# Moving the exponent tables of a two-layer spectral convolution to another stage, and the mirror differences to another engine

## The chip, the cores and the metric

The kernel runs on one core of a Trainium2 chip. The metric is the device time of one execution in microseconds (us). The core's engines are TensorE (PE; its weight loads are listed as PEld), VectorE (DVE), ScalarE (ACT), GpSimd (POOL) and SyncE (SP), which here only issues DMA transfers. All data is float32. L265 and the like are line numbers of the kernel before.

## The reference

Two layers act on x of shape 16 images x 16 channels x 256 x 256. The first normalizes groups of two channels and convolves (a 3x3 circular convolution); the second normalizes again and applies a Laplace-type operator, given by poles and residues: a steady part that mixes channels in the frequency domain, and a transient part built from exponentials along y and x.

```python
# layer 0
x = x + _L0_conv_ref(_gn(x), L0_conv_weight)
# layer 1
x = x + _L1_conv_ref(_gn(x), ty, tx, weights_pole1, weights_pole2, weights_residue)

def _L1_conv_ref(x, ty, tx, weights_pole1, weights_pole2, weights_residue):
    alpha = jnp.fft.fft2(x, axes=(-2, -1))
    A = 1.0 / (omega1[:, None, None, None] - weights_pole1[None])
    Bm = 1.0 / (omega2[:, None, None, None] - weights_pole2[None])
    S = jnp.einsum('ikpq,oikp,xikq->oxik', weights_residue, A, Bm)
    output_residue1 = jnp.einsum('biox,oxik->bkox', alpha, S)
    C = jnp.einsum('biox,oikp->bikpx', alpha, A)
    D = jnp.einsum('bikpx,xikq->bikpq', C, Bm)
    output_residue2 = jnp.einsum('bikpq,ikpq->bkpq', D, weights_residue)
    x1 = jnp.fft.ifft2(output_residue1, s=(Ny, Nx), axes=(-2, -1)).real
    E1 = jnp.exp(weights_pole1[..., None] * tyc)
    E2 = jnp.exp(weights_pole2[..., None] * txc)
    F = jnp.einsum('kbpq,bipz->kbiqz', output_residue2, E1)
    x2 = jnp.einsum('kbiqz,biqx->kizx', F, E2).real
    return x1 + x2 / Nx / Ny
```

E1 and E2 are the exponent tables of the change. They depend on the poles and on ty and tx alone, and the first place that reads them is the last stage of the kernel.

## The kernel before

The kernel has four stages. Each engine has its own queue of instructions, which it works through in order; within a queue the order follows the Python code closely, though the framework may move an instruction ahead of one that is not ready.

**Convolution.** The loop over `g` at L642 makes 24 steps for each of the 16 images, 387 in all. A step (`conv`, L251) issues 16 matmuls of 32x32 tiles at L265, recorded as 32. Every six steps a unit (`u`, four an image) of the layer's output, called v, is complete: ACT evicts its four row groups from PSUM with a bias at L280 into the `vt` tiles, of which there are four. Two steps later `mirror` (L230) forms the sum of the upper and the mirrored lower rows into `vsum` (two tiles; L232, DVE, which also accumulates the mean) and the difference in place (L235, DVE). ACT squares both for the variance (L243) four and five steps after `mirror`, and three steps after it SP stores both to `vD` in DRAM (L292, four transfers a unit). These delays are the numbers added to `g` in the lists `folded` and `squared`.

Beside this run the statistics of the images to come (`x_stats`, L159, bn_stats on DVE at L166, with due steps written out), the loads of x (`load_x`, L120: half an image in one transfer, issued by SP after steps 3 and 15 of an image for two images ahead, into five tiles), and two chains of table work: `make_poles`, `make_hat` (twice) and `make_c`, a piece every second step, and `make_exps` (twice) followed by `make_coef`, a piece every fourth step. `make_hat` and `make_c` have matmuls on PE (L443, L605).

**make_exps** (L473) makes a table for two channels at a time, in eight rounds: the phases on POOL (L490), their reduction to the range of the sine by rounding (L492 to L495, POOL) and subtraction in three parts (L501, DVE) and clamping (L504, L505, DVE), the exponentials on ACT (L491), the sine on ACT (L507), the product and two folds on POOL (L509, L511), and one or two stores to `eD` (L516). Exponential and sine need different activation tables, so each round has two loads of a table on ACT.

**Fold and forward transform.** 64 units of v are loaded (`load_v`, L694; the first by POOL, the others by SP), folded on DVE and POOL (L708 to L723) and transformed by PE (L730, L738, L773); spectra go to `aD`.

**Mixing.** The loop at L1109 runs over 32 groups of frequencies `g`, with four slots `n` each. A slot has the sums that make the weights of the next group (PE L981, evicted by ACT L996 and DVE L997), four blocks of 16 mixing matmuls (L1063, recorded as 64 a slot) into four PSUM banks `ps_mix`, their evictions into `yt` (L1120: three on ACT, one on DVE), the loads of the next group's spectra (`load`, L1037, four transfers in three slots of four) and the stores of `yt` to `yD` (`store`, L1075, four transfers). There are two `yt` tiles. `weights` (L918) makes the next weights on DVE and POOL (L952), a piece a slot. After group 2 `unmix_first` borrows a `yt` tile for the first group's repair.

**Inverse transform.** The last stage reads `yD`, `vD` and the tables in `eD`, and writes the output.

Of the kernel before, what the change touches and what calls it, by code (L numbers as in the profile page):

```python
# [9 lines left out]
FP = mybir.dt.float32  # L10
AF = mybir.ActivationFunctionType
# [13 lines left out]
def conv_then_laplace_kernel(ctx: ExitStack, tc: tile.TileContext, a: dict, out: bass.AP):  # L25
# [81 lines left out]
    p1 = ExitStack()  # L107
    wp = p1.enter_context(tc.tile_pool(name="conv_w", bufs=1))
    xp = p1.enter_context(tc.tile_pool(name="xt", bufs=5))
    vp = p1.enter_context(tc.tile_pool(name="vt", bufs=4))  # L110
    fp = p1.enter_context(tc.tile_pool(name="v_sums", bufs=2))
    jp = p1.enter_context(tc.tile_pool(name="junk", bufs=1))
    sp = p1.enter_context(tc.tile_pool(name="stats", bufs=2))
# [116 lines left out]
    def mirror(g, b, u, lo, hi):  # L230
        both = fp.tile([P, 2, 2, N], FP, name="vsum", tag="vsum")
        nc.vector.scalar_tensor_tensor(  # L232
            both, lo, 1.0, hi, ALU.mult, ALU.add, accum_out=sums[:, b, u : u + 1]
        )
        nc.vector.tensor_tensor(lo, lo, hi, ALU.subtract)  # L235
# [214 lines left out]
    def make_coef():  # L450


        rs = sw.tile([P, C, 4, 2], FP, name="s_rs", tag="s_th")
        nc.sync.dma_start(out=rs, in_=a["res_kq"])
        yield
        yield
        u = sw.tile([P, 4, C, 4], FP, name="s_u", tag="s_rn")
# [15 lines left out]
    def make_exps(which):  # L473


        pl = sw.tile([P, C, 2], FP, name="s_pl", tag="s_pl")
        nc.sync.dma_start(out=pl, in_=a[f"pole_e{which + 1}"])
        t = sw.tile([P, N], FP, name="s_t", tag="s_t")
        nc.sync.dma_start(out=t, in_=a[("ty", "tx")[which]].to_broadcast([P, N]))
        sign, phase, turns = (cols[:, 2 + 3 * which + j : 3 + 3 * which + j] for j in range(3))  # L480
        pim = sw.tile([P, C], FP, name="s_pim", tag="s_pim")
        nc.vector.tensor_scalar(pim, pl[:, :, 1], sign, None, ALU.mult)
        yield
        for q in range(8):
            th = sw.tile([P, 2, N], FP, name="s_th", tag="s_th")
            rn = sw.tile([P, 2, N], FP, name="s_rn", tag="s_rn")
            ex = sw.tile([P, 2, N], FP, name="s_ex", tag=f"s_ex{q % 2}")
            for j in range(2):
                i = 2 * q + j
                nc.gpsimd.tensor_scalar(th[:, j], t, pim[:, i : i + 1], None, ALU.mult)  # L490
                nc.scalar.activation(ex[:, j], t, AF.Exp, scale=pl[:, i, 0:1])  # L491
            nc.gpsimd.tensor_scalar(rn, th, 1.0 / (2 * PI), turns, ALU.mult, ALU.add)  # L492
            magic = 1.5 * 2.0**23
            nc.gpsimd.tensor_scalar(rn, rn, magic, None, ALU.add)
            nc.gpsimd.tensor_scalar(rn, rn, magic, None, ALU.subtract)  # L495
            yield
            c1 = 6.28125
            c2 = float(np.float32(1.93500518798828125e-3))
            c3 = 2 * np.pi - c1 - c2
            for c in (c1, c2, c3):  # L500
                nc.vector.scalar_tensor_tensor(th, rn, -float(c), th, ALU.mult, ALU.add)  # L501
                if c == c2:
                    yield
            nc.vector.tensor_scalar(th, th, phase, 3.1415925, ALU.add, ALU.min)  # L504
            nc.vector.tensor_scalar(th, th, -3.1415925, None, ALU.max)  # L505
            yield
            nc.scalar.activation(th, th, AF.Sin)  # L507
            yield
            nc.gpsimd.tensor_tensor(th, th, ex, ALU.mult)  # L509
            for op, eo in ((ALU.add, 0), (ALU.subtract, 1)):  # L510
                nc.gpsimd.tensor_tensor(  # L511
                    ex[:, :, eo * P : eo * P + P], th[:, :, 0:P], th[:, :, N - 1 : P - 1 : -1], op
                )
            yield
            for o in range(2 - which):
                nc.sync.dma_start(  # L516
                    out=eD[which][o, :, 2 * q : 2 * q + 2].rearrange("p i e t -> p i (e t)"),
                    in_=ex,
                )

    def make_c():

# [98 lines left out]
    def chain(*gens):  # L621
        for gen in gens:
            yield from gen
# [10 lines left out]
    for b in range(1, B):  # L634
# [36 lines left out]
    def pool(stage, name, bufs=1, **kw):  # L671
        return stage.enter_context(tc.tile_pool(name=name, bufs=bufs, reuse_waits="tile", **kw))
# [198 lines left out]
    g0 = pool(p2, "sg0")  # L871
    a0 = pool(p2, "abd0")
    wp = pool(p2, "w", 2)
    kp0 = pool(p2, "spare")
    kp = pool(p2, "m_const")
    up = pool(p2, "uv")
    a1 = pool(p2, "abd2")
# [16 lines left out]
    kp0.tile([P, 2304], FP, name="spare", tag="spare")  # L894

    zp.tile([P, 384], FP, name="between", tag="between")
    ct = tp.tile([P, 4, 8, N], FP, name="ct", tag="ct")
# [203 lines left out]

    p2.enter_context(tc.manual_schedule())
    accs = yp.tile([P, 2, B, 16], FP, name="accs", tag="yt")
    ahead, wt = first_sums()
    finish_projections()
    unmix = None
    for g in range(32):  # L1109
        sg, w_now = ahead, wt  # L1110
        steps = weights(g + 2) if g < 30 else iter(())
        ahead = new_sg(g + 1) if g < 31 else None
        for n in range(4):
# [4 lines left out]
            for m in range(4):  # L1118
                o, src = mix(4 * n + m, sg, yt)
                (nc.vector.tensor_copy if m == 3 else nc.scalar.copy)(o, src)  # L1120
            if g < 31:
                load(g + 1, n)
            store(g, n, yt)
            if n == 1 and unmix is not None:
                next(unmix, None)
                unmix = None
            wt = next_step(steps, None) or wt
        if g == 2:
            unmix = unmix_first()
            next(unmix)  # L1130
    p2.close()


# [358 lines left out]
```

## Time and profile before

| quantity | value |
|---|---|
| median of 3 runs | 2676.89 us (2670.39 to 2682.74) |
| the profiled execution's own time | 2679.43 us |
| its span on the core | 2677.6 us |
| mean granted TensorE clock | 0.982 |
| busy in the span: PE, DVE, ACT, POOL | 2508.3, 2029.9, 1480.2, 1014.6 us |
| DMA moved | 652.23 MB, mean 244 GB/s |
| convolution, first to last matmul | 26.2 to 613.3 us |
| fold, first matmul of L730 | 621.7 us |
| mixing, first to last matmul of L1063 | 1280.1 to 1901.4 us |

The profile is of one execution. Its lines give, for each group of instructions of the same line and shape, the busy time and the mean duration, and the idle time of the engine before them with what ended it. A wait is named after the instruction that came last, so it says what was late, not what was slow. A time on an engine that is not the bound costs nothing by itself; the chain of waits, followed back from the end, tells which engine was the bound where.

### The profile page before, as it was taken

What the parts mean: (1) busy time and instruction counts of PE and PEld (TensorE: products, weight loads), DVE (VectorE), ACT (ScalarE), POOL (GpSimd) and SP (SyncE); (2) the same over time, 40 slices, a digit from 0 to 9 for tenths busy, and PEclk for the clock granted to TensorE, in tenths of its full rate; (3) what the DMA queues carried; (4) which work ended last, traced back from release to release, by engine and by line L of the source; (5) the groups of instructions that cost most, each with busy time, mean ns of one, the idle gap of its engine ahead of it and who ended that gap; (6) DMA issues with size and microseconds to landing.
All of it is one profiled execution on the core that took longest, in us unless ns stands there. A gap on an engine that the chain in (4) does not pass through costs nothing.

```text
span 2677.6 us, 84178 instructions
## 1 busy us (share of the span) xinstructions
PE 2508.3 (94%) x35376; PEld 1861.7 (70%) x35376; DVE 2029.9 (76%) x3774; ACT 1480.2 (55%) x2772; POOL 1014.6 (38%) x988
## 2 busy tenths in 40 slices
PE   5888899898999999997989999999799999999998
PEld 2333444455777777774778888888678888888887
DVE  7777798967888888887777878787267666766666
ACT  4666687775666666664545555566334444444443
POOL 1333476612333333333200101010456565565753
PEclk9999999998999999998999999999899999999999
DMA  8777688855665666565667777777789899898995
GB/s 302 263 270 247 239 302 280 285 194 174 240 223 204 215 238 220 203 221 206 188 199 217 226 220 229 219 229 222 220 285 290 282 288 284 285 290 286 291 287 179
DMA packets 462729, 652.23 MB, mean 244 GB/s; under 512 B 49336, under 2 KB 425144, under 8 KB 448400
## 3 DMA queue, kind: packets, MB, share of 16 engines
q1 hardware_dynamic: 461280, 639.65, 73.6%
q8 instruction: 279, 4.57, 0.7%
q0 software_dynamic: 928, 3.02, 0.4%
q10 hardware_dynamic: 144, 4.19, 0.4%
q14 instruction: 98, 0.80, 0.1%
HBM read 367.22 MB, written 279.50 MB: 242 GB/s over the span
## 4 chain that ended last, share of the span: by engine, by line
PE 59%; DVE 12%; DMA 11%; POOL 5%; issue 5%; ACT 4%; SPq 4%; DVEq 0%; ACTq 0%; POOLq 0%
PE ps_mix L1063 11%; PE ps_y L730 9%; PE ps_y L738 8%; PE ps_p L1246 6%; PE ps_f L1270 5%; PE ps_f L1271 5%; PE ps_x L773 4%; DMA yD<-yt 4%; PE ps_conv L265 4%; PE ps_s L981 3%; DMA out_y<-ol 3%; DMA yk<-yD 2%; DVE xst L166 2%; SPq L1077 2%; DVE r L1279 2%
## 5 line engine op out<-in xcount | busy, mean ns | idle before, releaser
L1063 PEld LDWEIGHTS ps_mix<-abd,sg 128*64 128x64 f32 x8192 | 450.9, 138 | 74.3 <-ACT yt L1120 55.8
L1063 PE MATMUL ps_mix<-abd,sg 128*64 128x128 f32 x8192 | 481.9, 276 | 20.8 <-ACT yt L1120 20.6
L265 PE MATMUL ps_conv<-xt,wc 32*32 32x512 f32 x12288 | 459.0, 608 | 28.9 <-issue 17.7
L1210 POOL TENSOR_TENSOR u<-yk 128x512 f32<-128x512 f32 (+1 forms) x268 | 348.4, 1331 | 311.1 <-PE ps_p L1246 197.8
L746 ACT ACTIVATE t<-ps_y,vmr 128x384 f32<-128x384 f32 x512 | 298.1, 582 | 158.9 <-PE ps_y L738 158.8
L265 PEld LDWEIGHTS ps_conv<-xt,wc 32*32 32x32 f32 x12288 | 223.1, 104 | 216.7 <-issue 127.6
L997 DVE STREAM_SHUFFLE sg<-ps_s 128x512 f32<-128x512 f32 (+1 forms) x264 | 326.0, 1325 | 0.0
L1120 ACT COPY yt<-ps_mix 128x512 f32<-128x512 f32 x384 | 203.9, 600 | 214.8 <-DMA yD<-yt 174.5
L730 PE MATMUL ps_y<-tabE,vq 128*128 128x256 f32 x1024 | 313.5, 388 | 9.4 <-DVE vq L719 7.8
L738 PE MATMUL ps_y<-tabO,vq 128*128 128x256 f32 x1024 | 306.3, 381 | 0.0
L1270 PE MATMUL ps_f<-pt,inv 128*128 128x256 f32 x1008 | 300.6, 380 | 0.0
L1271 PE MATMUL ps_f<-hs,ey 128*128 128x256 f32 x1008 | 299.8, 379 | 0.0
L1246 PEld LDWEIGHTS ps_p<-inv,u 128*128 128x128 f32 x2048 | 265.6, 193 | 42.2 <-issue 24.7
L1274 DVE TENSOR_TENSOR r<-ps_f,q 128x256 f32<-128x256 f32 x256 | 107.0, 418 | 246.6 <-ACT q L1273 246.6
L1246 PE MATMUL ps_p<-inv,u 128*128 128x128 f32 x2048 | 279.1, 280 | 4.9 <-POOL u L1214 4.9
L952 POOL TENSOR_TENSOR w<-v,mcol 128x1024 f32<-128x1024 f32 x32 | 60.9, 1902 | 534.0 <-DVE v L942 534.0
L1273 ACT COPY q<-ps_f 128x256 f32<-128x256 f32 x256 | 95.6, 373 | 286.3 <-PE ps_f L1271 284.1
L730 PEld LDWEIGHTS ps_y<-tabE,vq 128*128 128x128 f32 x1024 | 189.8, 191 | 85.9 <-ACT q L786 50.3
L280 ACT ACTIVATE vt<-ps_conv,xq 128x512 f32<-128x512 f32 x256 | 160.6, 683 | 117.1 <-PE ps_conv L265 116.6
L1248 ACT COPY pt<-ps_p 128x512 f32<-128x512 f32 x256 | 150.5, 588 | 130.7 <-PE ps_p L1246 126.1
L738 PEld LDWEIGHTS ps_y<-tabO,vq 128*128 128x128 f32 x1024 | 195.7, 191 | 27.0
L1271 PEld LDWEIGHTS ps_f<-hs,ey 128*128 128x128 f32 x1008 | 191.5, 190 | 26.0
(232 smaller groups left out, 3822.6 us busy)
## 6 DMA issues: line engine op xcount, KB each, us to landing
xt<-in_x SPq DMA_DIRECT2D x31, 2322.0 KB, 9.6
yD<-yt SPq DMA_DIRECT2D x512, 128.0 KB, 3.2
vl<-vD SPq DMA_DIRECT2D x256, 256.0 KB, 3.8
out_y<-ol SPq DMA_DIRECT2D x128, 512.0 KB, 9.8
s<-vD SPq DMA_DIRECT2D x252, 256.0 KB, 6.4
aD<-spec SPq DMA_DIRECT2D x15, 4096.0 KB, 12.6
yk<-yD SPq DMA_DIRECT2D x60, 1024.0 KB, 8.3
vD<-vsum SPq DMA_DIRECT2D x128, 256.0 KB, 4.5
```

The lines of the kernel that those rows point to most:

```text
L265: nc.tensor.matmul(acc[r][32 * c : 32 * c + 32], lhsT=ready[b][0][rows, phase, tap], rhs=halves[b][u // 2][rows, q : q + 5 : 4, 2 - tap : ...
L280: nc.scalar.activation(vt[:, r % 2], acc[r], AF.Identity, bias=ready[b][1])
L730: nc.tensor.matmul(ps[:, 0:N], lhsT=vf[:, xo, 0, j], rhs=tabE[:, 0 : i + 2 : i + 1], start=True, stop=False, skip_group_check=True,)
L738: nc.tensor.matmul(ps[:, P : P + N], lhsT=vf[:, xo, 1, j], rhs=tabO[:, i : C + 1 : C - i], start=False, stop=True, skip_group_check=True,)
L746: nc.scalar.activation(t[:, xo, j].rearrange("p l n -> p (l n)"), ps[:, 0:384], AF.Copy, scale=vmr[:, 0, b0 + j, i : i + 1],)
L997: nc.vector.stream_shuffle(to[..., C + k : C + k + 2], src, swap)
L1063: nc.tensor.matmul(ps[64 * t : 64 * t + 64, j], lhsT=sg[:, f : f + 2].rearrange("p f m -> p (f m)"), rhs=abd[jq][:, :, 2 * t + cc, 2 * jj ...
L1120: (nc.vector.tensor_copy if m == 3 else nc.scalar.copy)(o, src)
L1210: nc.gpsimd.tensor_tensor(u[:, :, j].rearrange("p b (c n) -> p c b n", c=8), in0, in1, o)
L1246: nc.tensor.matmul(ps[:, at], lhsT=u[:, n], rhs=tab, start=True, stop=True)
L1270: nc.tensor.matmul(ps[:, e], lhsT=tab, rhs=pt[:, e], start=True, stop=False)
L1271: nc.tensor.matmul(ps[:, e], lhsT=ey[:, e], rhs=hs, start=False, stop=True)
```

## The change

The change has five parts.

- `make_exps` leaves the convolution's second chain, which keeps `make_coef` alone, and moves to the mixing stage. There, a piece is taken at the end of each slot from group 1 on. A round now has seven pieces instead of five (the exponentials have a piece of their own, after the reduction, and so has the store). All its DVE work goes to POOL: the three subtractions become a multiplication into a new tile and a subtraction each. Its tiles lie in a pool that takes the place of an unused one.
- In `mirror` the difference is made on POOL.
- In `mirror` the stores of v come six steps later instead of three, and the squares five and seven instead of four and five. There are six `vt` tiles instead of four; `vsum` keeps two.
- A half image of x is loaded in six transfers of three of its 18 rows (an x row here holds a pair) instead of one. The first half of image 0 keeps its own split.
- In a slot of mixing the store of `yt` is issued before the load of the next spectra.

```diff
-    vp = p1.enter_context(tc.tile_pool(name="vt", bufs=4))
+    vp = p1.enter_context(tc.tile_pool(name="vt", bufs=6))
...
-    def load_x(b, h, parts=(0, 18)):
+    def load_x(b, h, parts=range(0, 19, 3)):
...
-        nc.vector.tensor_tensor(lo, lo, hi, ALU.subtract)
-        folded.append((g + 3, b, u, (both, lo)))
-        squared.append((g + 4, lambda: square(both, 4 + 2 * u, b, bias=shift2[:, b : b + 1])))
-        squared.append((g + 5, lambda: square(lo, 5 + 2 * u, b)))
+        nc.gpsimd.tensor_tensor(lo, lo, hi, ALU.subtract)
+        folded.append((g + 6, b, u, (both, lo)))
+        squared.append((g + 5, lambda: square(both, 4 + 2 * u, b, bias=shift2[:, b : b + 1])))
+        squared.append((g + 7, lambda: square(lo, 5 + 2 * u, b)))
...
-        (4, 1, chain(make_exps(0), make_exps(1), make_coef())),
+        (4, 1, make_coef()),
...
+    def make_exps(which):
...
+        for q in range(8):
+            th = ep.tile([P, 2, N], FP, name="s_th", tag="s_th")
+            rn = ep.tile([P, 2, N], FP, name="s_rn", tag="s_rn")
+            tmp = ep.tile([P, 2, N], FP, name="s_tmp", tag="s_tmp")
+            ex = ep.tile([P, 2, N], FP, name="s_ex", tag="s_ex")
+            for j in range(2):
+                i = 2 * q + j
+                nc.gpsimd.tensor_scalar(th[:, j], t, pim[:, i : i + 1], None, ALU.mult)
+            nc.gpsimd.tensor_scalar(rn, th, 1.0 / (2 * PI), turns, ALU.mult, ALU.add)
+            magic = 1.5 * 2.0**23
+            nc.gpsimd.tensor_scalar(rn, rn, magic, None, ALU.add)
+            nc.gpsimd.tensor_scalar(rn, rn, magic, None, ALU.subtract)
+            yield
...
+            for c in (c1, c2, c3):
+                nc.gpsimd.tensor_scalar(tmp, rn, float(c), None, ALU.mult)
+                nc.gpsimd.tensor_tensor(th, th, tmp, ALU.subtract)
+                if c == c2:
+                    yield
+            nc.gpsimd.tensor_scalar(th, th, phase, 3.1415925, ALU.add, ALU.min)
+            nc.gpsimd.tensor_scalar(th, th, -3.1415925, None, ALU.max)
+            yield
+            for j in range(2):
+                i = 2 * q + j
+                nc.scalar.activation(ex[:, j], t, AF.Exp, scale=pl[:, i, 0:1])
+            yield
+            nc.scalar.activation(th, th, AF.Sin)
+            yield
+            nc.gpsimd.tensor_tensor(th, th, ex, ALU.mult)
+            for op, eo in ((ALU.add, 0), (ALU.subtract, 1)):
+                nc.gpsimd.tensor_tensor(
+                    ex[:, :, eo * P : eo * P + P], th[:, :, 0:P], th[:, :, N - 1 : P - 1 : -1], op
+                )
+            yield
+            for o in range(2 - which):
+                nc.sync.dma_start(
+                    out=eD[which][o, :, 2 * q : 2 * q + 2].rearrange("p i e t -> p i (e t)"),
+                    in_=ex,
+                )
+            yield
...
+    exps = chain(make_exps(0), make_exps(1))
...
+            store(g, n, yt)
             if g < 31:
                 load(g + 1, n)
-            store(g, n, yt)
...
             wt = next_step(steps, None) or wt
+            if g:
+                next(exps, None)
```

More of the change, by code (lines that the diff above doesn't have):

```diff
@@ L450, in make_coef @@
     def make_coef():
-        rs = sw.tile([P, C, 4, 2], FP, name="s_rs", tag="s_th")
+        rs = sw.tile([P, C, 4, 2], FP, name="s_rs", tag="s_rs")
         nc.sync.dma_start(out=rs, in_=a["res_kq"])
@@ L456, in make_coef @@
         yield
-        u = sw.tile([P, 4, C, 4], FP, name="s_u", tag="s_rn")
+        u = sw.tile([P, 4, C, 4], FP, name="s_u", tag="s_u")
         m0, m1 = cols[:, 0:1], cols[:, 1:2]
@@ L471, in make_coef @@
         yield
[L473 to L519, printed above, removed]
     def make_c():
@@ L873, in conv_then_laplace_kernel @@
     wp = pool(p2, "w", 2)
-    kp0 = pool(p2, "spare")
+    ep = pool(p2, "exps")
     kp = pool(p2, "m_const")
@@ L893, in conv_then_laplace_kernel @@
     ]
-    kp0.tile([P, 2304], FP, name="spare", tag="spare")
     zp.tile([P, 384], FP, name="between", tag="between")
@@ L1100, in unmix_first @@
             nc.sync.dma_start(out=at[:, c], in_=t[:, c])
+    def make_exps(which):
+        pl = ep.tile([P, C, 2], FP, name="s_pl", tag="s_pl")
+        nc.sync.dma_start(out=pl, in_=a[f"pole_e{which + 1}"])
+        t = ep.tile([P, N], FP, name="s_t", tag="s_t")
+        nc.sync.dma_start(out=t, in_=a[("ty", "tx")[which]].to_broadcast([P, N]))
+        sign, phase, turns = (cols[:, 2 + 3 * which + j : 3 + 3 * which + j] for j in range(3))
+        pim = ep.tile([P, C], FP, name="s_pim", tag="s_pim")
+        nc.gpsimd.tensor_scalar(pim, pl[:, :, 1], sign, None, ALU.mult)
+        yield
[12 more added lines that the diff above has]
+            yield
+            c1 = 6.28125
+            c2 = float(np.float32(1.93500518798828125e-3))
+            c3 = 2 * np.pi - c1 - c2
+            for c in (c1, c2, c3):
[23 more added lines that the diff above has]
+                )
+            yield
@@ L1130, in conv_then_laplace_kernel @@
             next(unmix)
+    for _ in exps:
+        pass
     p2.close()
```

## The prediction

> **What bounds the kernel now.** I read stages first, then the chain inside the stage that the change empties, then the waits of the stage that it fills. The table of stages gives each window's length, then the busy time of PE, PEld, DVE, ACT and POOL (with instruction counts), the clock, the DMA share and GB/s:
>
> ```profile
> 26.00:346.00 320.00, 274.37 (x6267) 129.74 (x6272) 247.89 (x459) 207.44 (x330) 128.98 (x106) 0.96 0.77 259
> 346.00:554.00 208.00, 191.69 (x4867) 92.90 (x4874) 189.87 (x329) 163.02 (x285) 138.40 (x142) 0.98 0.83 290
> 554.00:586.00 32.00, 29.06 (x815) 15.50 (x804) 23.40 (x59) 20.05 (x38) 1.26 (x1) 1.00 0.43 144
> 586.00:613.00 27.00, 26.68 (x798) 18.32 (x778) 9.91 (x13) 20.03 (x35) 3.17 (x4) 1.00 0.64 209
> 622.00:1240.00 618.00, 616.10 (x4092) 443.98 (x4095) 519.07 (x1186) 372.24 (x639) 219.93 (x282) 0.99 0.61 215
> 1280.00:1901.00 621.00, 600.24 (x12128) 510.61 (x12122) 474.29 (x871) 351.68 (x629) 65.31 (x39) 0.99 0.75 220
> ```
>
> The first four windows are the convolution. L265 has 12288 matmul records, 768 per image. The same table for L265 alone shows eight images in the first window (6137 records, 40.0 us each) and six in the second (4619 records, 34.7 us each); image 14 takes 32 us and image 15 takes 27:
>
> ```profile
> 26.00:346.00 320.00, 232.78 (x6137) 109.77 (x6142) 0.96 0.77 259
> 346.00:554.00 208.00, 172.27 (x4619) 81.24 (x4626) 0.98 0.83 290
> 554.00:586.00 32.00, 26.33 (x777) 13.77 (x766) 1.00 0.43 144
> ```
>
> Image 15 has neither statistics nor tables beside it and shows what PE needs: 27 us. Fold (622 to 1240) is full of PE work and untouched. In mixing (1280 to 1901) PE has only 21 us idle, DVE is at 76%, ACT at 57%, POOL at 11%. What fills an image of the convolution, the chain of waits shows (start, length, what):
>
> ```profile
> 354.33 1.10 DVE vsum L232 x2
> ...
> 355.45 1.30 DVE vt L235
> ...
> 360.44 1.23 DVE vt L235
> 361.67 0.61 DVE xst L166
> 362.27 1.65 DVE s_cden L573
> ...
> 371.86 1.51 DVE vt L235
> ```
>
> From 346 to 386 the chain is DVE almost alone; L235, the mirror difference, is 17.6% of it. Mixing's own waits (who, by whom, us, times, longest):
>
> ```profile
> ACT yt L1120 <- DMA yD<-yt: 165.6, 77, 7.1
> DVE yt L1120 <- DMA yD<-yt: 34.6, 31, 6.0
> PE ps_mix L1063 <- ACT yt L1120: 20.6, 21, 4.5
> ```
>
> ACT stands for 166 us until the stores of the two yt buffers have landed, and all of PE's idle time there waits for ACT. The removed work, by groups (busy, mean ns):
>
> ```profile
> L490 POOL TENSOR_SCALAR s_th<-s_t,s_pim 128x256 f32<-128x256 f32 x32 | 37.4, 1180 | 42.8 <-DVE s_pim L482 35.9 <-DMA s_t<-in_tx 6.4
> L509 POOL TENSOR_TENSOR s_th<-s_th,s_ex 128x512 f32<-128x512 f32 x16 | 24.5, 1533 | 112.9 <-ACT s_th L507 108.0 <-DMA xt<-in_x 4.9
> L491 ACT ACT_TABLE_LOAD x16 | 20.5, 1283 | 0.3
> L507 ACT ACT_TABLE_LOAD x16 | 20.5, 1283 | 3.8 <-DVE s_th L505 3.5
> ```
>
> **What the skill says.** The Trainium skill, "ScalarE: Activation LUTs", section "What ACT_TABLE_LOAD costs", gives 1283 ns for a load and about 1380 ns of drain before it. The trace agrees on 1283, but ACT is idle only 0.3 us before sixteen loads, so I charge no drain. "SBUF — State Buffer", section "Who interferes with whom", says that a DVE instruction with two SBUF inputs and a GpSimd one that reads SBUF lock each other out, while DVE with one SBUF input is free. In the trace L235 takes 1224 ns when POOL is idle and 1516 on average when POOL overlaps it (37 of 64); bn_stats stays at 673 to 678 either way. The lock is there, but costs about 0.3 us a meeting. "DMA: Bandwidth & Descriptors", section "Queues, rings and completion order", says that an engine consumes a ring's descriptors in ring order; the trace has an x transfer's packets occupying the engines for 7 to 8.5 us.
>
> **Part by part, convolution.** Per image, over the 13.2 images in which the exponent tables run, they take: DVE 50.6 us in all (L501 35.5, L504 8.0, L505 7.1), 3.8 an image; ACT 65.7 (loads 41.0, exponentials 14.6, sines 10.1), 5.0; POOL 156.9 (the six lines L490 to L511), 11.9. The difference takes 87.9/63 = 1.4 us of DVE, four times an image, 5.6. So in images 8 to 13 DVE falls from 31.6 (189.87/6) to 22.2 us, ACT from 27.2 to 22.2. POOL gets the difference: 128x512 on two SBUF inputs takes 1.27 us (L718), so 128x1024 is estimated at 2.5, 10 us an image; 23.1 becomes 21.4. That is not more than before, and POOL loses the 108 us for which it stood behind the sine. No compute engine but PE is left near 30 us. DMA moves 290 GB/s x 34.7 us = 10.1 MB an image, less 0.5 MB of table stores; at 32.2 us that is 298 GB/s, a share of about 0.85, near but not at the limit.
>
> PE then decides. All PE work but L265 is 41.6 us over images 0 to 7 (5.2 each) and 19.4 over 8 to 13 (3.2 each). L265 I take at 27.5 an image. Residual waits (statistics, table matmuls waiting for POOL) were 2.9 us in image 14, where DVE was already light; I keep 3.0 for the first eight, which hold the rational tables' chains, and 1.5 for the others. New: 5.2+27.5+3.0 = 35.7 against 40.0, 8 x 4.3 = 34 us; 3.2+27.5+1.5 = 32.2 against 34.7, 6 x 2.5 = 15; image 14, 1. Sum 50. Bounds: nothing, if each wait is replaced by another; 99 us, if all PE idle time (45.6+16.3+2.9) and all of L265 above 26.5 (21+13) goes.
>
> **Later stores.** A sum's store comes six steps after mirror, not three, and there are still two vsum buffers, so its landing must fit in six steps instead of nine: some 8 us instead of 12 at 1.35 us a step. Stores landed in 4.2 to 4.5 us at the median, 8.8 at most. But on SP two stores an image now sit behind an x half (issued at steps 3 and 15): about 2.4 us of issue, 8 of x data, 3 of landing make 13. DVE then waits about 4 us at the sum, and bn_stats behind it; 14 images x 2 x 4 = 112 us at worst. DVE has 9 us an image free, so I charge 6 us (0 to 50). The squares come one and two steps later, so ACT's 42 us of waiting for the sums before evictions mostly goes; it is inside the 50. The two more vt buffers pay for the longer hold.
>
> **x in six pieces.** Ten more SP issues of 0.4 us an image; SP is busy 35% there (69 of 200 us), and the bytes are the same. Pieces of 3096 B instead of 18576 cost the engines a few per cent of 5.5 us a half. bn_stats waited for x only 3 us in all, so little can be gained: 0 (-3 to +5).
>
> **Stage border.** The last difference ends on POOL about 1.3 us later than on DVE; the POOL load of the first v follows. In the trace that load went out at 601.7, ahead of the last images' stores. If it stays ahead, +1; if it falls behind the last difference, first fold work comes near 630 instead of 621.7, +8. I take +1.
>
> **Mixing.** 16 rounds of seven slots each, 112 of 124 slots of 4.67 us, so they end before the stage does. ACT: 1.283+2x0.503 in one slot, 1.283+0.632 in another, 4.2 us a round, 67 us in all. It is queued behind the slot's evictions and ahead of the next slot's. ACT works 2.8 us a slot, so 1.9 is free, and much of that was the wait for yt. A late first eviction has some 2.6 us before PE lacks a ps_mix bank, against 2.3 for the longer insert; I charge 8 us (0 to 67). POOL: from the minima 2x0.92+0.69+5x1.49+3x1.27+0.69+1.49+1.27+2x0.73 = 18.7 us a round, with contention 20, with weights (1.9 per four slots) 23.5 of 32.7; the sine's input is ready at about 19 us, when ACT arrives. DVE: seven two-input operations per four slots meet POOL perhaps 4.5 times at 0.35, 1.6 us of 18.7, 76% to about 85%: hidden, bound 20 us if each waits for a whole 1.5 us operation. SP issues 407 of 450 us between 1400 and 1850; 24 more stores at 0.5 are 12 us over the stage, just fitting.
>
> Stores before loads: a yt buffer's circle is copies 1.6, load issues 2.4, store issues 2.0, landing 3.2: 9.2 of the 9.33 us that two slots give. Without the loads it is 6.8. I credit 8 of PE's 21 idle us (the unmixing at slots 12 to 15 holds some 13 that stay); bounds 0 and 20. The loads, 2 us later, have three slots of slack. Mixing nets 0.
>
> **Sum** against the profiled execution (span 2677.6, time 2679.4, itself 2.5 above the median): -50+6+1+0 = -43, 2636; I forecast 2635.
>
> **Rivals and chances.** Half a per cent, 13 us, is about what can be told from no change.
> - Convolution falls to PE's limit with residual waits: 2635, chance 0.42, own range 2615 to 2655. For it: DVE's chain, light image 14.
> - It falls nearly to PE's bare need and yt's circle frees mixing: -75-5, 2600, 0.14. Against: PE's table matmuls wait for their own chain.
> - The two vsum buffers become the bound behind x: 35 us of the 112 reach PE through the statistics, 2679-50+35, about 2664, 0.22, evenly faster and same. For it: fewer steps to land; against: the free DVE time.
> - Slower: ACT's inserts in mixing are not hidden. All 67 us on PE gives 2679-43+59, about 2695; it decides from 51 of the 67 us, three quarters, and would show as PE waiting for L1120 after each exponential. For it: evictions already run late by the yt wait; against: the freed circle. 0.22, with DVE's lock and SP's fullness pushing the same way.
>
> Faster 0.66, same 0.12, slower 0.22. Range 2600 to 2695.
>
> **What would show it.** Right: convolution from 587 to about 543 us, with images 8 to 13 near 32; L166 and L235's successor off the chain; ACT's wait for yD well under 166 us; mixing within 10 us of 621. Wrong: DVE waiting for vD<-vsum, images still at 35; or a PE idle time of 2 us in two of seven slots; or fold starting near 630.

## The result, and the profile after

| | before | after |
|---|---|---|
| median of 20 runs each, us | 2677.48 | 2676.30 |
| lowest to highest, us | 2668.55 to 2682.74 | 2669.12 to 2691.99 |
| span of the profiled execution, us | 2677.6 | 2671.1 |

The ratio, which is not the quotient of the two medians, is 1.0012 with an interval of 0.9999 to 1.0026: no change in time. The forecast was 2635. The stages show that much happened all the same. Lengths are from first to last matmul of a stage, in the profiled execution; "border" is the time between the last convolution matmul and the first of the fold, "gap" that between fold and mixing, "rest" what follows the last mixing matmul.

| us | convolution | border | fold | gap | mixing | rest |
|---|---|---|---|---|---|---|
| before | 587.7 | 7.8 | 615.9 | 42.5 | 621.5 | 776.0 |
| after | 554.9 | 11.3 | 615.9 | 42.6 | 651.9 | 767.9 |
| difference | -32.8 | +3.5 | 0 | +0.1 | +30.4 | -8.1 |

So the convolution gave 33 us and mixing took 30 back. The differences add up to -7 us, where the medians differ by 1: the profiled execution of after lies 3 us below its median, that of before 2 us above. The table of stages of the kernel after has the same columns as the one shown of before: window, length, busy time of PE, PEld, DVE, ACT and POOL, clock, DMA share, GB/s. The first two windows are images 0 to 7 and 8 to 13; the next two are fold and mixing.

```profile
26.00:324.00 298.00, 269.99 (x6264) 132.67 (x6266) 193.75 (x414) 160.59 (x281) 103.66 (x60) 0.97 0.82 268
324.00:525.00 201.00, 189.26 (x4858) 92.24 (x4844) 135.70 (x260) 124.49 (x238) 117.87 (x110) 0.99 0.86 285
593.00:1209.00 616.00, 614.44 (x4068) 443.23 (x4068) 519.41 (x1186) 370.38 (x638) 219.90 (x282) 0.99 0.61 216
1251.00:1903.00 652.00, 603.51 (x12144) 511.40 (x12128) 485.08 (x872) 424.80 (x712) 386.98 (x297) 0.99 0.75 221
```

Images 8 to 13 now take 33.5 us each (201/6) with DVE busy for 22.6 of them, where it was 31.6. In mixing PE is busy as long as before (603.5 against 600.2), but its idle time went from 21 to 48.5 us. No engine is near full there: DVE has 74%, ACT 65%, POOL 59%. Mixing's loss is therefore waiting, not work, and the waits of PE in that stage say for what (who, by whom, us, times, longest):

```profile
PE ps_mix L1014 <- ACT yt L1126: 16.1, 10, 5.7
PE ps_mix L1014 <- DMA abd<-aD: 11.7, 10, 1.7
PE ps_s L932 <- POOL w L903: 6.7, 3, 3.3
PE ps_mix L1014 <- DVE sg L948: 6.2, 4, 1.8
PE ps_mix L1014 <- ACT sg L947: 3.7, 3, 1.5
```

Lines moved with the change: L1014 is the mixing matmul (L1063 before), L1126 the eviction into `yt` (L1120), L932 and L903 the sums and the weights (L981, L952), L947 and L948 the evictions of the sums. Before, the first line, with 20.6 us, was all there was. Now PE also waits for spectra (`abd`), for weights that POOL makes, and for sums that are evicted late. ACT's own wait for stores of `yt`, 165.6 us before, fell as forecast, and another of the stage's waits is new:

```profile
ACT yt L1126 <- DMA yD<-yt: 69.0, 34, 7.8
POOL s_pim L1064 <- DMA s_pl<-in_pole_e: 33.2, 2, 18.8
```

The second line is two waits only: POOL stood up to 18.8 us for the poles, the first thing that a set of tables reads. The chain of waits of after goes through one of them (start, length, what):

```profile
1558.65 1.41 POOL s_ex L1098 x2
1560.06 18.70 issue
...
1578.83 0.14 POOL s_pim L1064
1578.96 0.16 issue
1579.12 1.90 POOL w L903
1581.02 0.04 issue
1581.07 1.91 PE ps_s L932 x32
```

The timeline of the same moment shows what the 18.7 us are. SP comes to the load of the poles only at 1574.68, in its order of slots, and POOL had been there since 1560:

```profile
1574.04 0.60 SPq L996 DMA_DIRECT2D abd<-aD  x1
...
1574.68 0.59 SPq L1059 DMA_DIRECT2D s_pl<-in_pole_e  x1
...
1578.83 0.33 POOL L1064 TENSOR_SCALAR s_pim<-s_pl,cols 128x16 f32<-128x16 f32 x1 [18.77 <-DMA s_pl<-in_pole_e]
1579.12 1.89 POOL L903 TENSOR_TENSOR w<-v,mcol 128x1024 f32<-128x1024 f32 x1
...
1581.07 1.91 PE L932 MATMUL ps_s<-ct,w 64*32 64x256 f32 x32 [3.25 <-POOL w L903]
```

Behind the standing instruction in POOL's queue are the mixing weights of the next group. They are done 2.2 us after it is released, and PE has by then been idle for 3.25. PE pays for such a wait twice. In the 3.4 us that follow this wait, and the one for the poles of the first set, the granted clock is about half (windows of after, with the clock third from the end):

```profile
1291.00:1294.40 3.40, 3.18 (x44) 1.97 (x46) 0.39 (x2) 1.13 (x2) 3.15 (x4) 0.51 0.77 231
1581.00:1584.40 3.40, 3.33 (x46) 2.23 (x48) 0.64 (x2) 1.30 (x2) 3.20 (x5) 0.53 0.81 247
```

### The profile page after: what moved, and what is told of

It reads as the page before. It is cut to its first block, busy times and chain, and to the rows that moved or that the text cites. A ratio compares the mean times of both kernels' runs of the same rounds, so it can differ in the third digit from the quotient of the medians.

```text
span 2671.1 us, 84484 instructions
## 1 busy us (share of the span) xinstructions
PE 2504.5 (94%) x35376; PEld 1867.1 (70%) x35376; DVE 1912.9 (72%) x3628; ACT 1465.3 (55%) x2758; POOL 1306.7 (49%) x1182
## 4 chain that ended last, share of the span: by engine, by line
PE 47%; DMA 14%; DVE 8%; SPq 4%; issue 2%; POOL 2%; ACT 1%; DVEq 0%; ACTq 0%; POOLq 0%
PE ps_mix L1014 11%; PE ps_y L682 9%; PE ps_y L690 8%; DMA out_y<-ol 5%; PE ps_x L725 4%; DMA yk<-yD 4%; PE ps_p L1256 3%; PE ps_f L1280 3%; PE ps_f L1281 3%; PE ps_s L932 3%; DMA yD<-yt 3%; DVE r L1289 2%; DVE ol L1291 2%; DVE ol L1292 2%; DMA abd<-aD 1%
## 5 line engine op out<-in xcount | busy, mean ns | idle before, releaser
L1014 PE MATMUL ps_mix<-abd,sg 128*64 128x128 f32 x8192 | 481.6, 276 | 41.8 <-ACT yt L1126 16.1
L1014 PEld LDWEIGHTS ps_mix<-abd,sg 128*64 128x64 f32 x8192 | 450.9, 138 | 96.9 <-issue 39.7
L1220 POOL TENSOR_TENSOR u<-yk 128x512 f32<-128x512 f32 (+1 forms) x268 | 342.9, 1310 | 317.6 <-PE ps_p L1256 209.9
L265 PE MATMUL ps_conv<-xt,wc 32*32 32x512 f32 x12288 | 457.1, 612 | 28.5 <-issue 28.4
L265 PEld LDWEIGHTS ps_conv<-xt,wc 32*32 32x32 f32 x12288 | 229.5, 104 | 207.6 <-issue 149.1
L948 DVE STREAM_SHUFFLE sg<-ps_s 128x512 f32<-128x512 f32 (+1 forms) x264 | 326.1, 1325 | 0.0
L682 PE MATMUL ps_y<-tabE,vq 128*128 128x256 f32 x1024 | 313.5, 388 | 12.9 <-DVE vq L671 11.3
L235 POOL TENSOR_TENSOR vt<-vt 128x1024 f32<-128x1024 f32 x64 | 152.4, 2382 | 325.7 <-DVE vsum L232 241.7
L1126 ACT COPY yt<-ps_mix 128x512 f32<-128x512 f32 x384 | 210.7, 591 | 120.4 <-DMA yD<-yt 69.0
L947 ACT ACTIVATE sg<-ps_s,mcol 128x512 f32<-128x512 f32 (+1 forms) x264 | 167.3, 685 | 106.9 <-PE ps_s L932 106.9
L670 POOL TENSOR_TENSOR vq<-vf 128x512 f32<-128x512 f32 x64 | 81.4, 1272 | 293.5 <-DVE vf L674 272.3
```

The lines of the kernel that those rows point to most:

```text
L265: nc.tensor.matmul(acc[r][32 * c : 32 * c + 32], lhsT=ready[b][0][rows, phase, tap], rhs=halves[b][u // 2][rows, q : q + 5 : 4, 2 - tap : ...
L682: nc.tensor.matmul(ps[:, 0:N], lhsT=vf[:, xo, 0, j], rhs=tabE[:, 0 : i + 2 : i + 1], start=True, stop=False, skip_group_check=True,)
L947: nc.scalar.activation(to[..., k : k + 2], src, AF.Copy, scale=nsgn)
L948: nc.vector.stream_shuffle(to[..., C + k : C + k + 2], src, swap)
L1014: nc.tensor.matmul(ps[64 * t : 64 * t + 64, j], lhsT=sg[:, f : f + 2].rearrange("p f m -> p (f m)"), rhs=abd[jq][:, :, 2 * t + cc, 2 * jj ...
L1220: nc.gpsimd.tensor_tensor(u[:, :, j].rearrange("p b (c n) -> p c b n", c=8), in0, in1, o)
```

## The experiments

Sixteen kernels were run. All stages in us, from one profiled execution each; "idle" is the time in mixing in which PE does nothing, 20.8 us in before and 48.5 in after; ratios are to the kernel before, with 95% intervals.

| kernel | convolution | border | mixing | idle | rest | ratio |
|---|---|---|---|---|---|---|
| e1 after, load before store | 552.3 | 11.3 | 645.4 | 35.1 | 776.9 | 1.0001 [0.9987, 1.0015] |
| e2 before, store before load | 585.5 | 7.8 | 617.6 | 21.7 | 767.9 | 1.0003 [0.9989, 1.0018] |
| e3 before, tables moved | 554.8 | 7.8 | 642.9 | 36.0 | 775.5 | 0.9969 [0.9958, 0.9981] |
| e4 e1 with DVE differences | 550.6 | 6.9 | 642.1 | 36.8 | 777.1 | 0.9958 [0.9945, 0.9971] |
| e5 e3, one ACT table | 564.0 | 7.8 | 641.4 | 37.0 | 774.2 | 0.9975 [0.9961, 0.9988] |
| e6 e3, no ACT work | 556.4 | 7.8 | 638.8 | 33.1 | 775.5 | 0.9961 [0.9945, 0.9977] |
| e7 e3, a third of POOL's work | 554.1 | 7.8 | 642.0 | 35.3 | 776.8 | 0.9964 [0.9946, 0.9981] |
| e8 e4, x in one transfer | 548.6 | 6.9 | 645.5 | 39.0 | 771.7 | 0.9962 [0.9947, 0.9977] |
| e9 e3, table loads ahead | 558.4 | 7.8 | 631.3 | 28.7 | 774.7 | 0.9939 [0.9918, 0.9961] |
| e10 e3, no table stores | 555.5 | 7.8 | 635.1 | 32.7 | 776.5 | 0.9941 [0.9923, 0.9959] |
| e11 e3, table stores by POOL | 553.3 | 7.8 | 640.6 | 33.8 | 770.7 | 0.9960 [0.9943, 0.9977] |
| e12 e4 with e9 and e11 | 550.9 | 6.9 | 634.8 | 29.5 | 775.9 | 0.9899 [0.9873, 0.9925] |
| f13 after, table loads ahead | 555.5 | 11.8 | 645.8 | 46.3 | 765.3 | 0.9962 [0.9949, 0.9975] |
| f14 e12, one load first | 547.2 | 6.9 | 626.2 | 27.9 | 772.9 | 0.9893 [0.9874, 0.9911] |
| f15 e9, no table stores | 552.6 | 7.8 | 622.9 | 23.5 | 771.6 | 0.9894 [0.9876, 0.9911] |
| f16 e9, no ACT work | 555.0 | 7.8 | 633.1 | 32.9 | 769.0 | 0.9937 [0.9920, 0.9954] |

How far may one such length be trusted? Nine kernels (e3, e5 to e7, e9 to e11, f15, f16) have the same convolution code and show 552.6 to 564.0, median 555.0. Four (e1, e3, e4, e8) have the same mixing code and show 642.1 to 645.5, mean 644.0. Their idle times are 35.1 to 39.0, mean 36.7. A difference below 4 us of mixing says nothing by itself, and of the convolution, where the nine span 11 us, not even that. The two columns don't always agree, for the length also holds PE's work at a lower clock: between the first and the last matmul of mixing the granted clock is half for 3.4 us in e2, f14 and f15, 13.7 in before, 17.1 in after and 27.3 in e1 and e6. In the 8 us before each such stretch PE had stood idle for 1.9 to 4.8 us.

The first theory after the result (theory 1 below) was the order of store and load in mixing, against theory 2, the work on the tables itself. Later, theory 2 was divided: ACT's inserts (A), POOL's work and its lock with DVE (B), the tables' stores on SP's queue (C) and POOL standing in its queue behind loads that SP issues late (D).

**The order of store and load.** In e1 the change keeps everything but this, in e2 the kernel before gets this alone.

```diff
-            store(g, n, yt)
             if g < 31:
                 load(g + 1, n)
+            store(g, n, yt)
```

> The changed kernel with the load of the next spectra put before the store of yt again. Theory 1 (the order is the loss): SP now issues the load of the tile that the next group's first slot reads some 3.7 us after the slot that frees it instead of 0.2 us, its last transfer lands just as PE needs it, and the fourth slots of the groups are 30 us longer for it. Undone, mixing falls from 652 to 620-630 us, the issue comes back to about 0.2 us after the slot, and the time falls by 22 to 30 us, ratio to before 0.988 to 0.993. Theory 2 (the exponent rounds themselves are the loss, through ACT's inserts, POOL and 24 more stores on SP): mixing stays at 645 or more and the time within 8 us of before.

> The kernel before with one part of the change alone: the store of yt ahead of the load in a mixing slot. Theory 1: mixing goes from 621 to 640-650 us, all of it in the fourth slots, ratio 1.007 to 1.011. Theory 2: without the exponent rounds the order is harmless or helps, as the forecast had it: mixing 610 to 622, ratio 0.995 to 1.001. Between the two: the order costs only together with the rounds' stores on SP.

In e1 mixing fell to 645.4, not to near 621, and with three other kernels of that code to a mean of 644.0: the order costs about 8 us of the 30 when tables are made beside it, and 12 of PE's idle time. In e2, without tables, mixing is 617.6, 4 us shorter than before, which is not more than the scatter, and the time is the same. Its waits of PE show why the new order brings nothing even there:

```profile
PE ps_mix L1063 <- DMA abd<-aD: 11.7, 11, 2.4
PE ps_mix L1063 <- ACT yt L1120: 8.7, 4, 3.7
```

The wait for ACT is 12 us shorter than the 20.6 of before, and a wait for spectra of the same size stands in its place. All of these waits, here and in after, are at the first matmul of a group. Theory 1 is a part of the loss in mixing and no more. In the whole time it isn't seen: after and e1 differ by 2 us in their medians and their intervals overlap, for in the profiled executions the rest is 9 us longer in e1 (more on this below).

**Which part made the convolution's gain.** e3 is the kernel before with the tables moved, and nothing else; e4 is e1 with the difference back on DVE; e8 is e4 with x in one transfer.

```diff
# e4
-        nc.gpsimd.tensor_tensor(lo, lo, hi, ALU.subtract)
+        nc.vector.tensor_tensor(lo, lo, hi, ALU.subtract)
```

> The kernel before with the exponent tables moved to mixing and nothing else (load before store, differences on VectorE, old squares and stores, x whole). Theory 1: mixing lengthens by 0 to 8 us, and the convolution shortens by 20 to 30 us, ratio 0.990 to 0.995. Theory 2: mixing lengthens by 20 us or more, ratio 0.998 to 1.003.

> The changed kernel with load before store and the mirror differences back on VectorE. If the differences on GpSimd gave a good part of the convolution's 32 us, the convolution is 8 us or more longer than with them (562 us and more, first to last matmul, against 555); if the tables alone gave it, it is within 4 us, and the stage border, 11.3 us after and 7.8 before, falls back to about 8.

> e4 (the changed kernel with load before store and the differences on VectorE) with x in one transfer a half again. If the six pieces are neutral, as forecast, the convolution stays at 549-553 us and the ratio at 0.995-0.997, and the 4 us between e3 (554.8) and e4 (550.6) are the later squares and stores; if the pieces gave them, it goes back to 554-556.

e3 has a convolution of 554.8, after 554.9: moving the tables is the whole gain. Its chain of waits over the stretch where the one of before was DVE almost alone begins:

```profile
by line: PE ps_conv L265 82.1%; PE ps_setup L557 11.5%; issue 4.2%; PE ps_stat L178 3.1%
```

PE holds the chain there, with the difference still on DVE. Putting it on POOL costs: the three kernels with POOL differences and later stores (after, e1, f13) have 554.2 on average, the three with DVE differences, later stores and x in pieces (e4, e12, f14) 549.6, and their borders are 11.5 and 6.9. That is 9 us, and e1 and e4 differ by 11.8 us in their medians (2674.03, 2662.24). Later stores and squares with six `vt` tiles take the convolution from the median of 555.0 to 548.6 in e8, some 6 us; the pieces of x, between e8 and those 549.6, nothing. The four kernels with both later stores and DVE differences, 547.2 to 550.9, all lie below the nine, but the whole times of e3 and e4 don't show the 6 us.

**ACT's inserts and POOL's work.** e5 makes copies of exponentials and sines, so no table is loaded and the tables hold other values. e6 leaves exponentials and sines out. e7 leaves out the reduction of the phases but for one operation, two thirds of POOL's table work, with a tile of the same size in place of the two that go.

```diff
# e6
-            for j in range(2):
-                i = 2 * q + j
-                nc.scalar.activation(ex[:, j], t, AF.Exp, scale=pl[:, i, 0:1])
             yield
-            nc.scalar.activation(th, th, AF.Sin)
             yield
-            nc.gpsimd.tensor_tensor(th, th, ex, ALU.mult)
+            nc.gpsimd.tensor_tensor(th, th, rn, ALU.mult)
# e7
-            nc.gpsimd.tensor_scalar(rn, th, 1.0 / (2 * PI), turns, ALU.mult, ALU.add)
...
-            nc.gpsimd.tensor_scalar(th, th, -3.1415925, None, ALU.max)
```

> The kernel with only the exponent tables moved (e3), and in their rounds exponential and sine replaced by plain copies of the same size, so that no activation table is loaded (the tables hold other values; every other instruction stays). Theory A, ACT's inserts are what costs mixing its 21 us (621.5 before, 642.9 in e3): with 41 of their 67 us gone, mixing falls to 622-630. Theory B, the rounds' work on GpSimd is what costs (the lock against VectorE's two-input operations, the weights queued behind it): mixing stays at 638-645.

> e3 without the rounds' exponential and sine (left out, with their loads; the product takes another factor, so the tables hold other values). Theory A: mixing returns to 619-625 us, as before. Theory B: 638-645.

> e3 with the reduction of the sine's argument left out but for one operation: 4 GpSimd instructions fewer for the rounding and 7 fewer for subtraction and clamp, about 13 of 19 us a round; exponential, sine, product, folds and stores stay (the tables hold other values). Theory A: mixing stays at 638-645 us. Theory B: it falls to 622-630. If neither A nor B moves it, the 24 stores on SP are what is left.

Mixing stays at 641.4, 638.8 and 642.0, against 644.0. Neither A nor B came true. Neither ACT's table loads nor POOL's load on DVE make the loss; for all of ACT's work some 5 us are left.

**POOL behind its own loads; the tables' stores.** e9 loads the poles of both sets and the first times ahead of the mixing loop, and the second times before the last sine of the first set. e10 leaves the tables' stores out of mixing (three large stores of other values fill `eD` in the fold stage), e11 has POOL issue them.

```diff
# e9
-        pl = ep.tile([P, C, 2], FP, name="s_pl", tag="s_pl")
+    pls = []
+    for which in range(2):
+        pl = ep.tile([P, C, 2], FP, name=f"s_pl{which}", tag=f"s_pl{which}")
         nc.sync.dma_start(out=pl, in_=a[f"pole_e{which + 1}"])
+        pls.append(pl)
...
+            if which == 0 and q == 7:
+                ahead_of.append((pls[1], load_t(1)))
             nc.scalar.activation(th, th, AF.Sin)
# e11
-                nc.sync.dma_start(
+                nc.gpsimd.dma_start(
                     out=eD[which][o, :, 2 * q : 2 * q + 2].rearrange("p i e t -> p i (e t)"),
```

> e3 with the poles of both rounds' sets and the first times loaded ahead of the mixing loop, the second times three slots ahead, so that GpSimd doesn't stand in its queue for a late load with the mixing weights behind it. Theory D, those two waits are part of the loss (PE waits 5.2 us for the weights in e3, 7.7 in e6): mixing falls from 642.9 to 634-638 us. If they only hide other stalls: 641-644.

> e3 without the rounds' 24 stores in mixing (left out; the table memory is filled once in the fold stage with other values by three transfers). Theory C, the stores' place on SP, which was already issuing nine tenths of the time, lengthens the circle of the two yt tiles: mixing falls to 625-633 us. If SP and the stores are innocent too: 639-645, and what is left is the stage's shifted tiles or its start.

> e3 with the rounds' 24 stores issued by GpSimd instead of SP. Theory C with the place on SP as the cost: mixing 625-634 us. If it is the traffic of the stores that costs and not SP's time: 639-645 here, but 625-633 in e10.

e9 takes mixing to 631.3, further than expected. Its window, and then what is left in it of PE's waits for weights:

```profile
1250.00:1882.00 632.00, 603.13 (x12136) 509.23 (x12136) 482.50 (x873) 416.41 (x709) 387.71 (x297) 0.99 0.76 227
```

```profile
PE ps_s L932 <- POOL w L903: 0.5, 2, 0.4
```

POOL is busy for 388 us as before the edit, and the wait for the poles is gone: the 12.7 us (644.0 to 631.3) were paid for a place in a queue, not for work. Seven of them can be located. Groups 1 and 15, in which the poles are waited for, take 44.4 us together on average in the four kernels and 37.4 in e9, and PE's idle time falls by 8.0. In the six kernels that load the poles ahead (e9, e12, f13 to f16) the clock is never half in these two groups. e10 is worth 8.9 us (644.0 to 635.1), 4.0 of them idle time; e11 only 3.4, which is no more than the scatter.

**Is that all of it?** e12 puts the good parts together: e4 with e9's loads and e11's stores. f15 is e9 without the tables' stores (as e10), f16 is e9 without ACT's work (as e6), f13 the kernel after with the loads ahead.

> A version from the parts that help: e4 (load before store, differences on VectorE, later squares and stores, x in six pieces) with the loads ahead of e9 and the stores on GpSimd of e11. With theories C and D: mixing 622-630 us, convolution 549-553, ratio to before 0.988-0.992. Without them: 0.995-0.997, like e4.

> The changed kernel with e9's loads ahead and nothing else. If the GpSimd wait and the order are separate losses: mixing falls from 652 by 10-13 us to 639-643, still 8-12 above e9's 631, with PE waiting some 10 us for the abd loads at the first slots of groups. If the order hurt only through the GpSimd waits: 630-634 and no such waits.

> e9 without the rounds' 24 stores (as in e10, the table memory is filled with other values in the fold stage). If the stores on SP are the rest of the loss: 621-625 us of mixing against 631.3; if ACT's inserts are: 629-632.

> e9 without the rounds' exponential, sine and their loads (left out as in e6, the tables hold other values). If ACT's inserts are the rest of the loss: mixing 621-625 us against 631.3; if the stores are: 629-632.

f15 has the whole table work on ACT and POOL, and a mixing stage of 622.9:

```profile
1245.00:1869.00 624.00, 600.51 (x12160) 506.36 (x12144) 479.41 (x873) 417.69 (x709) 387.27 (x297) 1.00 0.74 219
```

Against 621.5 before, that leaves 1.4 us (2.7 of idle time), within the scatter, for all inserts on ACT, all work on POOL and the locks between POOL and DVE together. f16, which leaves ACT's part out, stays at 633.1, and e9 with it has 631.3. So there are three causes, undone one after the other: 8 us for the order of store and load, 13 for POOL behind its loads, and 8 for the tables' stores, 29 of the 30. e12, whose stores POOL issues, is at 634.8, above the 622 to 630 expected and not below e9: within the scatter the stores cost the same from either queue. Whether their price lies in their transfers or in both queues was not told apart.

The sizes depend on what is undone first. In f13, where POOL's wait goes first, mixing is still 645.8, 3 us above the range expected: this step brings 6.1 us, 7.8 in groups 1 and 15, and the order, undone after it, 14.5 (f13 against e9). f13's waits of PE:

```profile
PE ps_mix L1014 <- ACT yt L1138: 16.3, 7, 7.7
PE ps_mix L1014 <- DMA abd<-aD: 16.0, 13, 2.7
PE ps_mix L1014 <- ACT sg L947: 10.4, 8, 1.9
```

The whole times bear out two of the three. By their ratios POOL's loads are worth some 13 us in f13 (against after) and 8 in e9 (against e3), the stores 12 in f15 (against e9) and 8 in e10 (against e3). For f13 and f15 the intervals lie apart, for e9 and e10 they just meet. For the order the whole times show nothing.

**A better order.** The load in slot 1 is the one that comes due first, for it brings the spectra of the next group's slots 0 and 1 alike. In after PE waited for this load by itself 11.0 us (instruction and line that waited, us, times):

```profile
L996 SPq DMA_DIRECT2D abd<-aD x124: 516/601/1618, 1262.6 to 1874.5; - x124
...
  PE ps_mix L1014: 11.0, 9
```

f14 is e12 with this load ahead of the store, and the other two behind it.

```diff
-            if g < 31:
+            if n == 1 and g < 31:
                 load(g + 1, n)
             store(g, n, yt)
+            if n != 1 and g < 31:
+                load(g + 1, n)
```

> e12 with the store before the load in all slots but the second, where the load stays first: that load fills the tile that the next group's first slot reads. If this one load is how the order costs, the first slots wait for no abd load, and the freed circle of yt shows: mixing 624-631 us against 634.8 in e12, ratio 0.985-0.989. If not: 635-642.

In f14 PE waits for no spectra, though most stores go first, unlike in f13 with its 16.0 us; e12, with all loads first, has no such wait either. Mixing falls from 634.8 in e12 to 626.2, with the tables in it. PE's waits in mixing, and the windows of convolution and mixing:

```profile
PE ps_mix L1014 <- ACT yt L1138: 16.6, 16, 3.0
PE ps_s L932 <- POOL w L903: 4.2, 3, 1.7
PE ps_mix L1014 <- DVE yt L1138: 4.0, 5, 0.9
```

```profile
27.00:574.00 547.00, 512.08 (x12702) 259.80 (x12686) 412.85 (x772) 326.88 (x593) 116.06 (x124) 0.98 0.82 269
1238.00:1865.00 627.00, 599.06 (x12164) 506.88 (x12152) 485.63 (x875) 418.05 (x709) 401.69 (x322) 1.00 0.76 228
```

The median is 2645.84 us beside 2675.39 of the kernel before, a ratio of 0.9893 (0.9874 to 0.9911): about 1% faster than before, and so than after, from the same idea. That this one load gives the 8.6 us is not shown, though. Only 1.6 us of them are idle time. They lie in group 3, the one with the repair (32.5 us in e12, 27.3 in f14), and in the last (20.1, 15.5), while the other thirty take 1.2 us more. Group 3 may well be the order's work, for the four kernels that put stores first there take 26.9 to 27.9 us and twelve of the fourteen others 28.0 to 32.5. The medians of e12 and f14 (2649.48, 2645.84) aren't told apart, and the profiled execution was the slowest of its six in e12 and the second fastest in f14. Nearly all of the 1% is e12's already. In f14 the tables are moved, the stores and squares come later, the difference stays on DVE, the tables' first loads are ahead of the stage, and the one urgent load goes ahead of the store.

## Why the prediction was wrong

The forecast's sum was -50+6+1+0 = -43; the measured stages give -33 in the convolution, +3.5 at the border, +30 in mixing and -8 in the rest.

- **"Mixing nets 0"** is the step that failed, by 30 us, in three places. "The loads, 2 us later, have three slots of slack": not so. The load in slot 1 holds the spectra of the very first slot, and in after PE waits for it in nine of the groups; the order, credited with 8 us of gain, costs 8 (and 14.5 in f13 against e9). For POOL the working counted busy time, 20 us a round, and the rounds took (386.98 - 65.31)/16 = 20.1. That it fits is luck in part: the addition with minimum (L1087) was taken at 0.69 us and took 2.01, and that filled what was set aside for contention. The working didn't ask what the first instruction of each table set waits for. Two loads that SP issues in its own order of slots held up the weights in POOL's queue: 6 to 13 us. SP "just fitting" 24 more stores was put at nothing and was 8 us, and POOL as the issuer of the stores took none of it away.
- **ACT's inserts, 8 us (0 to 67)**, and with them the slower rival: f15 has them all and is 1.4 us above the mixing stage of before. That rival fell, though the stage it named did lose. **DVE's lock with POOL, hidden**: right, by the same run.
- **The circle of `yt`** opened as worked out: ACT's wait for its stores fell from 165.6 to 69.0 us, though a part of that is ACT's added work (e3, in the old order, has 113.9). PE's wait for ACT fell with it, by 12 us in e2, more than the 8 credited, but the late spectra took 11.7 us of that back: PE's idle time is 20.8 us in before and 21.7 in e2.
- **Convolution, "PE then decides"**: right in kind, e3's chain shows it; 50 less 6 forecast, 33 measured. The term that was mis-sized is L265 at 27.5 us an image. In after it takes 29.0 in images 0 to 7 and 28.5 in 8 to 13, no nearer to image 15 than before:

```profile
26.00:324.00 298.00, 232.10 (x6134) 113.55 (x6136) 0.97 0.82 268
324.00:525.00 201.00, 171.07 (x4610) 80.81 (x4596) 0.99 0.86 285
```

  That is 8 x 1.5 + 6 x 1.0 = 18 us. The 27.5 was taken close to image 15, in which the clock was full (1.00). About half of the 18 us, an estimate, is clock: in images 0 to 13 of after L265 was at work for 18.2 us while the granted clock was half, and at full clock that would have taken some 9. The working had no term for it. PE's idle time of 3.5 and 2.0 us an image, where 3.0 and 1.5 were taken, adds 7; PE's other work came out 5 lower. Matmul ends are modelled, so busy and idle are told apart only roughly, their sum exactly. The other half of L265's excess stays open.
- **The difference on POOL** was priced well (2.5 us; 2382 ns measured) and valued wrongly. The 5.6 us of DVE that it frees in an image bring nothing once the tables are gone: after has the convolution of e3. With POOL's difference e1 is slower than e4 by 11.8 us.
- **Later stores, +6, and the rival of two `vsum` buffers**: wrong in sign. Sums were stored in 2.8 us at the median, where they took 4.5, and the waits of the convolution in after have them once, and not on DVE:

```profile
POOL vt L235 <- DVE vsum L232: 241.7, 43, 44.3
...
POOL vt L235 <- DMA vD<-vsum: 5.8, 1, 5.8
```

  With DVE differences the later steps, squares and two more tiles together bring about 6 us of the stage (e8).
- **x in pieces, 0**: right. The same bytes kept each DMA engine busy for 215 us in pieces (e4) and 203 whole (e8), 6% more, and the stage didn't notice.
- **Border, +1**: 3.5 in after, and 4.6 between kernels that differ in the difference's engine. The forecast named the cause, the load of the first v in POOL's queue. In after POOL issues four of these loads at 580.82, behind the next-to-last difference, so neither of the two cases that the forecast named came about in full; in e4 two are out at 567.60. The timelines of the two, first after, then e4:

```profile
578.52 2.38 POOL L235 TENSOR_TENSOR vt<-vt 128x1024 f32<-128x1024 f32 x1 [3.97 <-DVE vsum L232]
...
580.82 3.16 POOL L649 DMA_DIRECT2D s<-vD  x4
```

```profile
567.60 1.45 POOL L649 DMA_DIRECT2D s<-vD  x2
```

- **The rest, not in the sum**: 765 to 777 us, with the same code in that stage. Five of the 8 us are one wait, some 40 us into the rest. Before has it, after doesn't:

```profile
PE ps_h L1230 <- DVE r L1275: 5.1, 1, 5.1
```

  Of the eighteen kernels the eleven with this wait have a rest of 772.9 to 777.2 us, the seven without it 765.3 to 771.6. Three of the seven have all stores first (after, e2, f13: 765.3 to 767.9), four all loads (e8, e11, f15, f16), so the order alone doesn't decide on the wait. What does was not settled.

## What to carry to other kernels

When work is moved into a stage, do not ask only whether its engine has room: look at the first instruction of each piece, what it waits for, on whose queue that load is issued, and what stands behind the waiting instruction. Before two transfers on a queue change places, find the one that is due soonest, by what reads it first; with one urgent load ahead of the store PE waited for no spectra. And give each part of a change a run of its own, and look at PE's idle time beside a stage's length: here the moved tables made the whole gain and also, by their loads and stores, half of the loss in mixing or more, the difference on POOL cost 12 us more, and the sum looked like no change.

## What was unexpected of the hardware

- What a POOL tensor-scalar of 128x512 takes doesn't go by the number of its operations. In the timeline of after it is 0.69 us with multiplication and addition (L1074), 1.49 to 1.50 with one operation (L1076, L1077, L1083, L1088), 2.01 with addition and minimum (L1087).
- PE's short waits cost it more than their length: after two waits of 3.3 us for POOL's weights the granted clock was 0.51 and 0.53 over the next 3.4 us.
- A small load can stall an engine for far longer than its transfer: the poles are 16 KB, and POOL waited 18.8 and 14.4 us for them. Of the 18.8 us, 14.6 went by until SP came to the issue.
- Sharing SBUF between POOL and DVE cost nothing measurable in mixing: with POOL busy for 387 of 624 us and DVE for 479 (f15), where POOL had 65 us before, the stage was 1.4 us longer.
